# A state-space mixer rewritten: from a pipeline over chunks of 128 tokens to all chunks of 64 tokens at once

## The chip, the cores and the metric

The kernel runs on one core of one Trainium2 chip. The metric is the device time of one execution in microseconds, the median of several runs. Engines are named as in the profile: PE (TensorE matmul), PEld (TensorE weight load), DVE (VectorE), ACT (ScalarE), POOL (GpSimd), SP (SyncE, which here issues DMAs only).

## The reference, cut to what matters

The input is 8 images of 32x32 pixels and 128 channels in float32, or 8 sequences of 1024 tokens. Layer 0 is an attention over group-normalised tokens. Layer 1 adds a state-space mixer and then a spectral filter. Only the mixer is changed. It is computed twice for each sequence, forwards and backwards, each direction with its own weights, and both outputs are added:

```
z, xbc, dt = split(x @ in_proj, [256, 256 + 384])   # x: layer-normed tokens, 128 channels
xbc = silu(causal_conv4(xbc) + conv_b)
xh, Bm, Cm = split(xbc, [256, 256 + 64])            # 4 heads of 64; state size 64
dt = softplus(dt + dt_bias);  A = -exp(A_log)
# for each head, a linear recurrence over the tokens, written in chunks of CHUNK = 64:
#   Y_diag: inside a chunk,  C_l . B_s * exp(sum of dt*A from s+1 to l) * (xh*dt)_s,  s <= l
#   states: what a chunk adds to the 64x64 state, decayed to the chunk's end
#   Y_off : C_l . (state before the chunk) * exp(sum of dt*A up to l)
y  = Y_diag + Y_off + xh * D
yg = y * silu(z)
out = (yg * rsqrt(mean(yg^2) + 1e-5) * norm_w) @ out_proj
```

The result doesn't depend on the length of a chunk.

## The kernel before, in words

`fast_kernel` goes through stages, each with its own pools of SBUF and PSUM tiles: group norm and q, k, v of all images; attention (`scores`, `weigh`, `total`, `project`); the mixer; then the spectral filter in several stages (`spectra`, `matrices`, `apply`, `gather`, `back`). The tokens of all sequences stay in SBUF tiles `X[b]`, 128 tokens on the partitions and 8 blocks of tokens. A second program, `general_kernel`, follows for inputs outside a range that the fast one can handle; it isn't entered here and isn't changed.

A scheduling layer takes the written program, keeps its order as priority, gives out tile buffers and sets semaphores. So instructions of one engine may stand in another order than in the text, but each engine works through its own list in order.

The mixer has 16 units, one for each sequence and direction, direction 0 before 1. For a unit, `inputs` makes what the scan needs:

- once per sequence, `tokens`: layer norm, transposes to channels on partitions (`bxt`), the matmul for dt (`pd`), softplus in small DVE and ACT steps, `da` = dt*A;
- the decays `dec` (`pe`, L638, and an exponential);
- the projection of the 384 convolved channels in three tiles (`pp`, L654), each followed by a copy to `xp` and a scaled copy to `xs` or `bc` on ACT and three multiply-adds on DVE (L670);
- `z` with tokens on partitions (`pz`, L679), and the Silus (L694 to L697).

`scan` then does one chunk of 128 tokens at a time: transposes of x and B (`sx`), `xdt` on DVE, `xd`, `dau` and `xdd` on POOL, the segment sums `pl` (L735) and their exponential `lm` (L737), C.B (`pg`), its mask and product with `lm` (L742, L743), the new state (`pst`, L753, then POOL and DVE L758, L759), the outputs `sy` inside the chunk (L764) and from the state (L766), their sum and gate (L768 to L772), the sum of squares and `rms`, transposes back (`pyt`, L782) and the output matmul `spo` (L789) added to `X` (L790). The state goes from chunk to chunk.

The order is written out by hand: `scan` is a generator with four parts, and the chunks run as a pipeline, also across the end of a unit, with one part of the next unit's `inputs` behind each chunk:

```
            for n in range(NT):
                running = step([scan(b, d, n, made, state)] + running)
                for _ in range(2 if n == 0 else 1):
                    next(ahead, None)
```

PSUM is split among tags: `p` (one buffer of two banks, for `pp`, `pz`, `px`), one buffer each for `yt`, `x`, `seq` and `y`, two for `g`.

Of the kernel before, what the change touches and what calls it, by code (L numbers as in the profile page):

```python
# [8 lines left out]
F32 = mybir.dt.float32  # L9
# [5 lines left out]
P = 128  # L15
# [7 lines left out]
KC = 4  # L23
KF = 16
# [13 lines left out]
def fast_kernel(ctx: ExitStack, tc: tile.TileContext, a: dict, out: bass.AP, bad: bass.AP):  # L38
# [41 lines left out]

    row_le = triangle("row_le", -1, 1, 0)
    row_ge = triangle("row_ge", 1, -1, 0)
    row_lt = triangle("row_lt", -1, 1, -1)
    row_gt = triangle("row_gt", 1, -1, -1)
# [32 lines left out]
    win, cw, cb, wo, dsk = [], [], [], [], []  # L117
# [4 lines left out]
    def load_ssm_weights():  # L122
        for d, pre in enumerate(("L1_attn_fwd_", "L1_attn_bwd_")):
            w = ctile([P, 2 * DI + 2 * DS], f"win{d}")
            nc.sync.dma_start(w, a[pre + "in_proj"][:, : 2 * DI + 2 * DS])
            nc.sync.dma_start(wdt[:, d, :], a[pre + "in_proj"][:, 2 * DI + 2 * DS :])
            win.append(w)
            t = ctile([P, 3, KC], f"cw{d}")
            nc.sync.dma_start(t, a[pre + "conv_w"].rearrange("(n p) k -> p n k", p=P))
            cw.append(t)  # L130
            t = ctile([P, 3, 1], f"cb{d}")
# [4 lines left out]
            t = ctile([P, NH], f"dsk{d}")  # L136
            nc.sync.dma_start(t, a[pre + "D"].partition_broadcast(P))
            dsk.append(t)
# [209 lines left out]
    with ExitStack() as s:  # L348
        keepq = s.enter_context(tc.tile_pool(name="a_q", bufs=1))
        qs, ks, vs = [], [], []  # L350
        with ExitStack() as s2:
# [79 lines left out]
            load_ssm_weights()  # L431
# [72 lines left out]
        def project(b, half, av, pd):  # L504
# [4 lines left out]
            ot = p1.tile([P, 512], F32, tag="ot", name=f"ot{b}_{half}")  # L509
# [57 lines left out]

    with ExitStack() as s:
        p1 = s.enter_context(tc.tile_pool(name="b_1", bufs=1))
        p2 = s.enter_context(tc.tile_pool(name="b_2", bufs=2))  # L570
        p3 = s.enter_context(tc.tile_pool(name="b_3", bufs=3))
        ps_p = s.enter_context(tc.tile_pool(name="b_ps_p", bufs=1, space=PSUM))
        ps_1 = s.enter_context(tc.tile_pool(name="b_ps_1", bufs=1, space=PSUM))
        ps_2 = s.enter_context(tc.tile_pool(name="b_ps_2", bufs=2, space=PSUM))

        n2 = 2 * NH

        def tokens(b, seq):

            xn = layer_norm(p1, b, "b")  # L580
            px = ps_p.tile([P, T], F32, tag="p", name=f"px{b}")
            for j in range(NT):
                nc.tensor.transpose(px[:, j * P : (j + 1) * P], xn[:, j, :], ident)
            xt = p2.tile([P, T], F32, tag="xt", name=f"bxt{b}")
            nc.scalar.copy(xt, px)
# [3 lines left out]
            pd = ps_1.tile([P, NT * n2], F32, tag="yt", name=f"pd{b}")  # L589
            for j in range(NT):  # L590
                nc.tensor.matmul(
                    pd[:, j * n2 : (j + 1) * n2],
                    lhsT=xt[:, j * P : (j + 1) * P],
                    rhs=wdt.rearrange("p d h -> p (d h)"),
                    start=True,
                    stop=True,
                )
# [9 lines left out]
            nc.vector.tensor_tensor(v, pd.rearrange("p (j n) -> p j n", j=NT), wide(dtb), ALU.add)  # L607
# [17 lines left out]
        def inputs(b, d, seq, made):  # L625
# [5 lines left out]
            heads = slice(d * NH, (d + 1) * NH)  # L631
            upto, after = (row_le, row_gt) if d == 0 else (row_ge, row_lt)

            pe = ps_1.tile([P, 3, NT * NH], F32, tag="yt", name=f"pe{tag}")
            dac = p2.tile([P, NT, NH], F32, tag="dac", name=f"dac{tag}")
            nc.gpsimd.tensor_copy(dac, da[:, :, heads])
            for i, m in enumerate((upto, after, ones)):
                nc.tensor.matmul(  # L638
                    pe[:, i, :], lhsT=m, rhs=dac.rearrange("p j h -> p (j h)"), start=True, stop=True
                )  # L640
            dec = p2.tile([P, 3, NT, NH], F32, tag="dec", name=f"dec{tag}")
            nc.scalar.activation(
                dec.rearrange("p i j h -> p (i j h)"), pe.rearrange("p i n -> p (i n)"), AF.Exp
            )
            yield
# [3 lines left out]
            bc = p1.tile([P, T], F32, tag="bc", name=f"bc{tag}")  # L649
            pad = KC - 1  # L650
            for n, acc in ((0, xs[:, 0, :]), (1, xs[:, 1, :]), (2, bc)):
                pp = ps_p.tile([P, T], F32, tag="p", name=f"pp{tag}_{n}")
                for i in range(2):
                    nc.tensor.matmul(  # L654
                        pp[:, i * 512 : (i + 1) * 512],
                        lhsT=win[d][:, DI + n * P : DI + (n + 1) * P],
                        rhs=xt[:, i * 512 : (i + 1) * 512],
                        start=True,
                        stop=True,
                    )  # L660
# [6 lines left out]
                )  # L667
                for i in range(pad):
# [6 lines left out]
            zs = p2.tile([P, NT, DI], F32, tag="zs", name=f"zs{tag}")  # L675
            for j in range(0, NT, 4):
                pz = ps_p.tile([P, 4, DI], F32, tag="p", name=f"pz{tag}_{j}")
                for i in range(4):
                    nc.tensor.matmul(  # L679
                        pz[:, i, :],  # L680
                        lhsT=xt[:, (j + i) * P : (j + i + 1) * P],
                        rhs=win[d][:, 0:DI],
# [3 lines left out]
                nc.vector.tensor_copy(  # L686
                    zs[:, j : j + 4, :].rearrange("p j c -> p (j c)"), pz.rearrange("p j c -> p (j c)")
                )
                yield


            bt = p2.tile([DS, T], F32, tag="bt", name=f"bt{tag}")
            ct = p2.tile([DS, T], F32, tag="ct", name=f"ct{tag}")
            nc.scalar.activation(bt, bc[0:DS, :], AF.Silu)  # L694
            nc.scalar.activation(ct, bc[DS : 2 * DS, :], AF.Silu)
            for t in (xs.rearrange("p n t -> p (n t)"), zs.rearrange("p j c -> p (j c)")):
                nc.scalar.activation(t, t, AF.Silu)  # L697
            made.update(dt=seq["dt"], dec=dec, dac=dac, xs=xs, bt=bt, ct=ct, zs=zs)

        def split(t):  # L700
            return t.rearrange("p (h c) -> p h c", h=NH)

        def per_head(t, n=P):
            return t.unsqueeze(2).to_broadcast([n, NH, HP])

        def scan(b, d, n, made, state):

            dec, dac, xs, bt, ct = (made[k] for k in ("dec", "dac", "xs", "bt", "ct"))
            heads = slice(d * NH, (d + 1) * NH)
            upto, after = (row_le, row_gt) if d == 0 else (row_ge, row_lt)  # L710
            j = n if d == 0 else NT - 1 - n
            tag = f"{b}_{d}_{j}"
            cols = slice(j * P, (j + 1) * P)

            px = ps_1.tile([P, DI + DS], F32, tag="x", name=f"sx{tag}")
            for i in range(2):
                nc.tensor.transpose(px[:, i * P : (i + 1) * P], xs[:, i, cols], ident)
            nc.tensor.transpose(px[:, DI:], bt[:, cols], ident[:DS, :DS])
            xb = p2.tile([P, DI + DS], F32, tag="xb", name=f"xb{tag}")
            nc.scalar.copy(xb, px)  # L720
            xh = split(xb[:, :DI])
            xdt = p2.tile([P, DI], F32, tag="xdt", name=f"xdt{tag}")
            nc.vector.tensor_tensor(split(xdt), xh, per_head(made["dt"][:, j, heads]), ALU.mult)  # L723
# [1169 lines left out]
```

## Time and profile before

| | us |
|---|---|
| median of 3 runs | 1970.18 (1969.39 to 1972.31) |
| the profiled execution, own time | 1988.78 |
| its span | 1987.1 |
| mean granted TensorE clock | 0.918 |
| group norm, q, k, v (0 to 124) | 124, clock 0.88 |
| attention (124 to 511) | 387, clock 0.99 |
| mixer, start (511 to 548) | 37, clock 0.76 |
| mixer, units (548 to 1501) | 953, clock 0.90 |
| spectral filter (1501 to 1987) | 486 |

The profiled execution is 0.9% longer than the median of the runs; durations are taken from it. In a line of the timeline the first number is the start of a group of like instructions in us from the start of the span, the second is the time to the end of the last of them. A line of a group names line, engine and operation, output<-inputs, shapes and count. A line of waits reads: engine and its instruction, what it waited for, us in total, times, longest us. In a line of windows the numbers behind the length are busy us (and instructions) of PE, PEld, DVE, ACT and POOL, then the granted clock, the busy share of the DMA engines and GB/s.

### The profile page before, as it was taken

What the parts mean: (1) busy time and instruction counts of PE and PEld (TensorE: products, weight loads), DVE (VectorE), ACT (ScalarE), POOL (GpSimd) and SP (SyncE); (2) the same over time, 40 slices, a digit from 0 to 9 for tenths busy, and PEclk for the clock granted to TensorE, in tenths of its full rate; (3) what the DMA queues carried; (4) which work ended last, traced back from release to release, by engine and by line L of the source; (5) the groups of instructions that cost most, each with busy time, mean ns of one, the idle gap of its engine ahead of it and who ended that gap; (6) DMA issues with size and microseconds to landing.
All of it is one profiled execution on the core that took longest, in us unless ns stands there. A gap on an engine that the chain in (4) does not pass through costs nothing. (4 is left out here: it accounts for less than half of the span.)

```text
span 1987.1 us, 38739 instructions
## 1 busy us (share of the span) xinstructions
PE 1758.5 (88%) x15734; PEld 1060.3 (53%) x15734; DVE 1370.0 (69%) x2427; ACT 1051.9 (53%) x1646; POOL 1033.4 (52%) x1335
## 2 busy tenths in 40 slices
PE   5689999999699899898988999989896889999996
PEld 3432222222355565555655556555555788777772
DVE  6757677666777767877678776877764447767764
ACT  2346666666475646656465564656635325444440
POOL 5348885000277666776666766766675552323220
PEclk7899999999798979989899898988987889999998
DMA  4011111000000000000000000000003851122118
GB/s 112 1 32 55 56 57 32 1 1 1 0 1 1 12 1 1 12 0 12 1 1 11 1 11 1 1 12 0 11 1 128 226 167 57 62 64 64 62 44 305
DMA packets 80835, 80.21 MB, mean 40 GB/s; under 512 B 7272, under 2 KB 65000, under 8 KB 79624
## 3 DMA queue, kind: packets, MB, share of 16 engines
q1 hardware_dynamic: 78536, 73.45, 12.1%
q10 hardware_dynamic: 2112, 4.19, 0.6%
q8 instruction: 126, 2.06, 0.4%
q14 instruction: 61, 0.50, 0.1%
HBM read 44.08 MB, written 33.55 MB: 39 GB/s over the span
## 5 line engine op out<-in xcount | busy, mean ns | idle before, releaser
L461 ACT ACTIVATE pr<-pt 128x1024 f32<-128x1024 f32 x256 | 248.1, 1021 | 125.8 <-PE pt L456 93.0
L973 ACT COPY gs<-pg 128x512 f32<-128x512 f32 x256 | 137.4, 589 | 174.8 <-PE pg L960 159.2
L485 DVE TENSOR_TENSOR two<-pr,pr 128x1024 f32<-128x1024 f32 x128 | 162.2, 1298 | 95.3 <-PE pd L496 95.3
L971 DVE COPY gs<-pg 128x512 f32<-128x512 f32 x256 | 164.6, 684 | 88.6 <-PE pg L960 83.8
L960 PE MATMUL pg<-taps,mst 32*128 32x128 f32 x4096 | 169.7, 294 | 27.1 <-DVE gs L971 20.7
L764 PEld LDWEIGHTS sy<-xdt,lm 128*128 128x128 f32 x1024 | 141.9, 212 | 75.1 <-issue 32.5
L764 PE MATMUL sy<-xdt,lm 128*128 128x64 f32 x1024 | 154.6, 299 | 24.6 <-DVE y L771 24.1
L960 PEld LDWEIGHTS pg<-taps,mst 32*128 32x128 f32 x4096 | 142.3, 194 | 57.6 <-DVE gs L971 23.4
L456 PE MATMUL pt<-q,k 32*128 32x512 f32 x1024 | 160.6, 643 | 4.8 <-DVE taps L332 3.5
L725 POOL TENSOR_TENSOR xd<-xb,dsk 128x256 f32<-128x256 f32 x128 | 118.8, 928 | 70.8 <-DVE y L771 42.6
L476 PE MATMUL po<-pr,v 128*32 128x512 f32 x1024 | 148.7, 603 | 0.0
L670 DVE SCALAR_TENSOR_TENSOR xs<-xp,cw,xs 128x1024 f32<-128x1024 f32 x96 | 145.8, 1525 | 2.5 <-ACT xs L665 2.5
L995 PE MATMUL py<-gs,u 128*32 128x128 f32 (+1 forms) x4096 | 140.9, 281 | 0.5 <-ACT half L1007 0.5
L982 POOL COPY u<-us 128x512 f32<-128x512 f32 x16 | 17.1, 1068 | 220.4 <-issue 208.8
L663 POOL MEMSET xp<- 128x3 f32 x48 | 4.6, 98 | 216.3 <-PE pf L548 186.6
L995 PEld LDWEIGHTS py<-gs,u 128*32 128x32 f32 (+1 forms) x4096 | 105.3, 105 | 16.0 <-issue 1.5
L771 DVE TENSOR_TENSOR y<-sy,xd 128x256 f32<-128x256 f32 x128 | 53.9, 421 | 82.2 <-POOL xd L769 69.7
L456 PEld LDWEIGHTS pt<-q,k 32*128 32x128 f32 x1024 | 52.8, 184 | 103.1 <-PE pt L456 40.2
L654 PE MATMUL pp<-bxt,win 128*128 128x512 f32 x192 | 101.1, 645 | 3.6 <-ACT xs L665 2.9
L746 POOL TENSOR_TENSOR xdd<-xdt,dec 128x256 f32<-128x256 f32 x112 | 89.6, 800 | 27.0 <-DVE xdt L723 24.7
L728 POOL TENSOR_TENSOR dau<-row_le,dac 128x512 f32<-128x512 f32 x64 | 75.3, 1178 | 53.5 <-PE pl L735 53.5
L743 DVE TENSOR_TENSOR lm<-lm,gm 128x512 f32<-128x512 f32 x128 | 101.8, 795 | 2.0 <-ACT lm L737 1.0
(271 smaller groups left out, 4031.4 us busy)
## 6 DMA issues: line engine op xcount, KB each, us to landing
ud<-sp SPq DMA_DIRECT2D x8, 1024.0 KB
us<-ud SPq DMA_DIRECT2D x16, 512.0 KB
yd<-sums SPq DMA_DIRECT2D x32, 256.0 KB
yt<-yd SPq DMA_DIRECT2D x6, 1024.0 KB
X<-in_x SPq DMA_DIRECT2D x8, 512.0 KB
part_p<-in_L_ffn_M_phi_plus SPq DMA_DIRECT2D x32, 128.0 KB
part_m<-in_L_ffn_M_phi_minus SPq DMA_DIRECT2D x32, 128.0 KB
xd<-X SPq DMA_DIRECT2D x8, 512.0 KB
```

Of the source, the lines that this page charges most:

```text
L456: nc.tensor.matmul(pt[:, i, :], lhsT=k[rows, j * P : (j + 1) * P], rhs=q[rows, cols], start=True, stop=True)
L461: nc.scalar.activation(pr[:, 2 * g : 2 * g + 2, :].rearrange("p i t -> p (i t)"), pt.rearrange("p i t -> p (i t)"), AF.Exp,)
L476: nc.tensor.matmul(po[rows, :], lhsT=vs[b][:, j, rows], rhs=pr[:, h, :], start=(j == 0), stop=(j == NT - 1))
L485: nc.vector.tensor_tensor(two, sums["pr"][:, 2 * g : 2 * g + 2, :], pr[:, 2 * g : 2 * g + 2, :], ALU.add)
L670: nc.vector.scalar_tensor_tensor(acc, xp[:, at : at + T], cw[d][:, n, i : i + 1], acc, ALU.mult, ALU.add)
L725: nc.gpsimd.tensor_tensor(split(xd), xh, per_head(dsk[d]), ALU.mult)
L743: nc.vector.tensor_tensor(lm, lm, gm.unsqueeze(1).to_broadcast([P, NH, P]), ALU.mult)
L764: nc.tensor.matmul(py[:, 0, hc], lhsT=lm[:, h, :], rhs=xdt[:, hc], start=True, stop=True)
L960: nc.tensor.matmul(pts[g][:, e, :], lhsT=mst[rows, n * 4 + e, :], rhs=taps[rows, cols].rearrange("p f q m i -> p (f q m i)"), start=True, ...
L971: nc.vector.tensor_copy(to, frm)
L973: nc.scalar.copy(to, frm)
L995: nc.tensor.matmul(py[t * 32 : t * 32 + 32 - 16 * m, q, :], lhsT=u[:, i, f, q, m:].rearrange("p k i b -> p (k i b)"), rhs=mats[:, f, q, m, ...
```

## The change

The mixer is written anew for chunks of 64 tokens (`L = 64`): two chunks stand on the 128 partitions, at 0 to 63 and 64 to 127, and each operation covers all 16 chunks of a unit.

- `scan` becomes `mixed`, which runs once for each unit. Units don't overlap except for `inputs` of the next, of which one part follows each part of `mixed`. All PSUM tiles have two banks and one tag with four buffers (`wide_psum`).
- Segment sums use a mask of 64 columns, half as many elements. The decay of C is no longer a factor on tokens after the matmul: exponentials `ec` with channels on partitions come from matmuls with ones (`pe`) and are multiplied by C.
- Matmuls of B, C, states and outputs become 64x64 tiles of the array: B back to tokens (`sb`), C.B (`pg`), states (`pst`), outputs inside a chunk and from the state (`sy`). Outputs have channels on partitions and are summed in PSUM: the D term first, as a matmul with a diagonal matrix `skip`, then the terms inside the chunk, then those from the states.
- The states of 15 chunk ends are a chain of DVE operations of 64 columns, two to a step; those that the other half of the partitions needs go there by four DMAs into `moved`.
- z has channels on partitions and its Silu reads PSUM. y needs no transpose; its sum of squares is a matmul of the squares with one column of ones.
- B and C are convolved in the projection: four matmuls with weights multiplied by the taps (`wbc`), made at the start by eight POOL products from two more loads each.
- Layer norm of the mixer is applied by ACT in place of DVE. D is loaded by four small DMAs per direction. `ot` of the attention is written over `av`. The store of `X[b]` to `xd` stands at the end of a sequence's second unit.

```diff
-    row_lt = triangle("row_lt", -1, 1, -1)
-    row_gt = triangle("row_gt", 1, -1, -1)
+    upto = []
+    for d, m in enumerate((row_le, row_ge)):
+        t = ctile([P, L], f"upto{d}")
+        for c in range(2):
+            rows = slice(c * L, (c + 1) * L)
+            nc.gpsimd.tensor_copy(t[rows, :], m[rows, rows])
+        upto.append(t)
+    after = [triangle("row_gt", 1, -1, -1), triangle("row_lt", -1, 1, -1)]
+    nc.gpsimd.memset(after[0][L:, :L], 0.0)
+    nc.gpsimd.memset(after[1][:L, L:], 0.0)
...
+            w = pool.tile([P, P], F32, tag="w_bc", name=f"w_bc{d}")
+            nc.sync.dma_start(w, proj[:, 2 * DI : 2 * DI + 2 * DS])
+            rows = pool.tile([P, P, KC], F32, tag="rows_bc", name=f"rows_bc{d}")
+            nc.sync.dma_start(rows, taps_bc[DI:].partition_broadcast(P))
+            t = ctile([P, KC, P], f"wbc{d}")
+            for k in range(KC):
+                nc.gpsimd.tensor_tensor(t[:, k, :], w, rows[:, :, k], ALU.mult)
...
-            ot = p1.tile([P, 512], F32, tag="ot", name=f"ot{b}_{half}")
+            ot = av
...
+        ps_w = s.enter_context(tc.tile_pool(name="b_ps", bufs=4, space=PSUM))
...
+            dau = p1.tile([P, NT, NH, L], F32, tag="dau", name=f"dau{tag}")
+            nc.gpsimd.tensor_tensor(
+                dau,
+                upto[d].unsqueeze(1).unsqueeze(1).to_broadcast([P, NT, NH, L]),
+                da[:, :, d * NH : (d + 1) * NH].unsqueeze(3).to_broadcast([P, NT, NH, L]),
+                ALU.mult,
             )
...
+            pb = wide_psum(f"pb{tag}", (T,))
+            for i in range(2):
+                for k in range(KC):
+                    at = i * 512 + (k if d == 0 else 2 * pad - k)
                     nc.tensor.matmul(
+                        pb[:, i * 512 : (i + 1) * 512],
+                        lhsT=wbc[d][:, k, :],
+                        rhs=xt[:, at : at + 512],
...
+            pes = [wide_psum(f"pe{tag}_{r}", (NT, 2, L)) for r in range(2)]
+            for i in range(2):
+                for c in range(2):
+                    for r in range(2):
+                        rows = slice(c * L, (c + 1) * L)
+                        nc.tensor.matmul(
+                            pes[r][rows, 4 * i : 4 * i + 4],
+                            lhsT=ones[rows, :L],
+                            rhs=dau[rows, 4 * i : 4 * i + 4, 2 * r : 2 * r + 2, :],
...
+            pss = [wide_psum(f"pst{tag}_{c}", (NT, 2, HP)) for c in range(2)]
+            for j in range(NT):
+                for c in range(2):
+                    for r in range(2):
+                        rows = slice(c * L, (c + 1) * L)
+                        nc.tensor.matmul(
+                            pss[c][r * L : (r + 1) * L, j],
+                            lhsT=bk[rows, j, :],
+                            rhs=xdd[rows, j, 2 * r : 2 * r + 2, :],
...
+            for k, (j, c) in enumerate(chunks[:-1]):
+                if k == 0:
+                    nc.vector.tensor_copy(state[:, 0], pss[c][:, j])
                 else:
+                    for h in range(2):
+                        nc.vector.scalar_tensor_tensor(
+                            state[:, k, h, :],
+                            state[:, k - 1, h, :],
+                            dec[:, c, j, h : h + 1],
+                            pss[c][:, j, h, :],
...
+                        nc.sync.dma_start(
+                            moved[to, ks[0] // 2 : ks[-1] // 2 + 1],
+                            state[r * L : (r + 1) * L, ks[0] : ks[-1] + 1 : 2],
+                        )
...
+            pys = [wide_psum(f"sy{tag}_{c}", (2, NT, L)) for c in range(2)]
+            for c in range(2):
+                for n in range(2):
+                    nc.tensor.matmul(
+                        pys[c][:, n],
+                        lhsT=skip[d][:, n, :],
+                        rhs=xs[:, n, :].rearrange("p (j c l) -> p c j l", j=NT, c=2)[:, c],
...
+            for j in range(NT):
+                for r in range(2):
+                    for c in range(2):
+                        rows = slice(c * L, (c + 1) * L)
+                        for h in range(2):
+                            nc.tensor.matmul(
+                                pys[c][h * HP : (h + 1) * HP, r, j, :],
+                                lhsT=xdt[rows, j, 2 * r + h, :],
+                                rhs=lm[rows, j, 2 * r + h, :],
...
+                        for h in range(2):
+                            nc.tensor.matmul(
+                                pys[c][h * HP : (h + 1) * HP, r, j, :],
+                                lhsT=state[rows, k, h, :] if r == c else moved[rows, k // 2, h, :],
+                                rhs=ec[rows, r, j, h, :],
...
+            for n in range(2):
+                sq = p2.tile([P, T], F32, tag="sq", name=f"sq{tag}_{n}")
+                nc.scalar.activation(sq, y[:, n, :], AF.Square)
+                sqs.append(sq)
+            yield
+            for j in range(NT):
+                for n in range(2):
+                    nc.tensor.matmul(
+                        pss[:, j : j + 1],
+                        lhsT=sqs[n][:, j * P : (j + 1) * P],
+                        rhs=ones[:, 0:1],
...
-            state = {}
-            for n in range(NT):
-                running = step([scan(b, d, n, made, state)] + running)
-                for _ in range(2 if n == 0 else 1):
-                    next(ahead, None)
+            for _ in mixed(b, d, made):
+                next(ahead, None)
             for _ in ahead:
                 pass
             made = coming
```

Between these stand, in `mixed`, `pl` and `lm` (two PSUM tiles of 1024 columns), the decays `pdec`, the transposes `sx` and `xdt`, `sb` and its copy `bk` on ACT, `pg`, `xdd` and the product of `lm` with the masked C.B (`gm`), all on DVE where they are elementwise; and behind the sums of squares `rms` on POOL, the 16 output matmuls `spo` and 8 additions to `X` on DVE.

## The prediction

> **What bounds the kernel now.** I read the page first, then busy time by stage (windows), the waits and the timeline of one unit. A unit is one sequence and direction of the mixer; there are 16.
>
> ```profile
> span 1987.1 us, 38739 instructions
> ## 1 busy us (share of the span) xinstructions
> PE 1758.5 (88%) x15734; PEld 1060.3 (53%) x15734; DVE 1370.0 (69%) x2427; ACT 1051.9 (53%) x1646; POOL 1033.4 (52%) x1335
> ```
>
> ```profile
> 511.00:548.00 37.00, 26.65 (x87) 15.74 (x87) 28.37 (x89) 19.11 (x21) 13.88 (x19) 0.76 0.00 1
> 548.00:1501.00 953.00, 869.26 (x3795) 543.21 (x3793) 700.32 (x1336) 552.75 (x928) 655.79 (x894) 0.90 0.02 5
> ```
>
> The columns are stretch, length, then PE, PEld, DVE, ACT and POOL busy, granted clock, DMA. The mixer is the 953 us from 548 to 1501, 59.6 us a unit, with PE busy 91% of it and DVE 73%. The DMA chain that ends the page lies after the change. PE's waits in this stretch:
>
> ```profile
> PE sy L764 <- DVE y L771: 24.1, 33, 1.5
> PE pst L753 <- POOL xdd L746: 20.6, 27, 1.6
> PE pst L753 <- POOL rms L103: 5.8, 13, 0.6
> ```
>
> These are small, so PE nearly sets the pace. Busy PE is not PE at its peak, so I price PE by distances between starts:
>
> ```profile
> 1247.65 1.02 PE L735 MATMUL pl<-dau,row_lt 128*128 128x512 f32 x2
> 1248.51 1.03 PE L679 MATMUL pz<-win,bxt 128*128 128x256 f32 x4
> 1249.37 0.61 PE L789 MATMUL spo<-wo,yts 128*128 128x128 f32 x4
> ...
> 1254.49 1.10 PE L764 MATMUL sy<-xdt,lm 128*128 128x64 f32 x8 [0.84 <-DVE y L771]
> 1255.53 0.70 PE L766 MATMUL sy<-state,ct 64*128 64x256 f32 x2
> ```
>
> A float32 matmul is two records. 512 columns take 0.86 us (1247.65 to 1248.51), 256 take 0.43; four of 64 columns with 128-wide weights take 1.04, 0.26 each, hardly less than one of 128 columns (0.22 to 0.27)[...]. Transposes are one record, 0.11 us. Narrow tiles behave otherwise:
>
> ```profile
> 1700.26 1.08 PE L995 MATMUL py<-gs,u 128*32 128x128 f32 x32
> 1701.27 1.17 PE L960 MATMUL pg<-taps,mst 32*128 32x128 f32 x32
> 1702.37 1.08 PE L995 MATMUL py<-gs,u 128*32 128x128 f32 x32
> ```
>
> Here 16 matmuls take 1.01 or 1.10 us, so four on four different tiles take 0.25 together, what one takes alone. Last, the granted clock:
>
> ```profile
> 955.10:958.60 3.50, 2.42 (x13) 1.27 (x12) 2.99 (x8) 2.14 (x6) 3.18 (x6) 1.00 0.00 0
> 965.40:968.80 3.40, 3.40 (x25) 2.59 (x23) 2.22 (x8) 0.80 (x2) 2.13 (x5) 0.99 0.00 0
> 968.80:972.20 3.40, 3.40 (x10) 1.77 (x9) 3.13 (x7) 1.25 (x4) 3.31 (x4) 0.50 0.00 0
> ```
>
> The clock is 1.0 or 0.5 in such pieces. The mixer's mean of 0.90 is a fifth of the time at half, 12 us a unit. It drops after pieces filled with small matmuls and gaps, though PE counts as busy.
>
> [...] the median of `two` is 1224. [...] the yd store at the end of the chain took 2.19.
>
> **The change part by part, for one unit.**
>
> *PE work before:* a step, all read in the same way, is sx 0.57, pl 0.86, pg 0.41, pst 0.58, sy 1.04 and 0.62, pyt 0.28, spo 0.54, in all 4.9, times 8 less a pst and a sy, 38; xBC projections 6 x 0.86 = 5.2, pz 3.4, decays 0.7, tokens 1.3. Sum 48.6 at full clock.
>
> *PE work after, full array:* pp 4 x 0.86, bc projection with the convolution in its weights 8, pz 4, pl 4, skip 4: 24 x 0.86 = 20.6; 16 transposes 1.7; 3 decays 0.7; 16 sums of squares of one column at 0.22, 3.5; 16 output matmuls 3.5; tokens 1.3. Sum 31.3. *64x64 tiles:* ones matmuls 8 of 512 columns, on two tiles in pairs of the same tile: 3.4 if all pair, 6.9 if none; I take 4.5. pst 8 groups of four at 0.25, 2.0. The 16 diagonal and 15 state groups have 64 columns: between 0.13 and 0.25, I take 0.13: 4.1. sb and pg 8 pairs each: 2.0. [...] Total 45 at full clock; were the tiles one after another at 0.22, 32+64+60+32 matmuls would be 41 instead of 8, and the total 80. So PE's work hardly falls; the 4-fold bc projection (+5.2) eats what tiles save.
>
> *Other engines:* POOL loses xd, xdd, dau per step and yo's sum (most of its 41 us a unit) and keeps dau, 2048 elements, four times 1.04 = 4.2, hidden a unit ahead. ACT loses most table loads (1.28 each, 53+30+15 of them); after: 16 passes near 1 us, bt/ct 2.4, two loads, 25 in all, not bounding. DVE: 9 convolution steps become 6 (1.27 each), zs copies go; total 34.
>
> *The path.* The pipeline across chunks goes. `mixed` holds four 2-bank PSUM buffers and single lm, xdt, state and y, so units don't overlap: only `inputs` of the next lies between. In the order in which the changed program stands, a unit is a chain:
> - head: pl 3.4, ones 4.5, then decays 0.7, a pp 1.7, sx 0.9, each behind the other in PE's queue (ec's exponentials, 2 x 1.02, run beside), to the first xdt: 11.3 with a hand-over.
> - DVE: xdt, xdd, lm 6 x 1.22, gm 0.68, six convolution steps of the next unit in between 7.6, first state 0.3, then 14 dependent steps of two 64-column operations. X L790, 128 columns from PSUM, is 0.34; half the columns less 0.07 us, 0.27: 28 make 7.6. Sum 23.5. PE does pst, pb, pz under this. Behind each DVE step queue the next unit's convolutions, so ACT's Silu and pz wait with them.
> - tail: the second output buffer is a pst buffer, free only at the last state; skip 1.7, diagonal 2.1, states 2.0 (the DMAs of `moved`, 2.2, land under the first two; on SP nothing else is queued but the xd store), y 2 x 1.22, square 1.05, then sums and output 7.0, hand-overs between engines 8 x 0.15. Sum 17.5.
>
> Together 52.3; where tokens of the next sequence come in, px 0.9, pd 1.8 and the softplus go ahead of the convolutions, +3.3, so 54.0 on average, at full clock.
>
> *Clock.* In the tail PE is idle for y and square (3.5), then does one-column matmuls (3.3): two pieces that earn half clock. Nothing here shows this pattern; bounds 0 and 20 us at half, of which half is lost. I take 10, so +5.0: 59.0 a unit.
>
> *Ends of the stage.* Silu of the first xs ended at 542 in the trace, so the first xdt, at 11.3 of its chain, puts its start at 531. The last unit has no next: 7.6 of convolutions and 2 of waits less. End: 531 + 16 x 59.0 - 10 = 1465 against 1501, -36.
>
> *Elsewhere.* The weight products, 8 on POOL at about 0.5 (wo, double size, 0.7), and 8 more issues on SP (0.45 each) stand in the first 40 us, ahead of POOL's rsqrt of the next image. POOL has gaps of 3 to 4 us there: +2, bounds 0 and 6. The skip tables and chunk rows, some 2 us on POOL ahead of the first layer norm, are inside the rounding of 531. `ot` in `av`: the next copy into av comes 8 score steps (23 us) later, so 0. xd stores: one per sequence before and after, 0.
>
> Sum: -34 on the profiled execution's own 1988.8, or 1955; the median of the runs, 1970.2, is 0.9906 of it, so 1936.
>
> **The rivals.** A measurement tells 0.2% from no change, 4 us.
> 1. *Clock and hand-overs eat it* (slower). Break-even is (1501 + 10 - 531 - 2)/16 = 61.1 a unit, 7.1 above the full-clock chain: 14 us at half clock in PE's head and tail. The before has 12. For: the idle tail is longer than any wait now, and only one unit is in flight. Against: 512-column matmuls fill the middle. With 10 lost, 64, +46: 2015.
> 2. *The 64x64 tiles overlap only by halves* (slower). Chain +7 for diagonal, states and ones: 66, +78: about 2047; with no overlap +23, near 2300. For: not in the trace; the order mixes r and c. Against: 32-wide tiles overlap fully both ways.
> 3. *The clock holds* (faster): 55 a unit, -98: 1873.
> 4. *Nothing moves:* PE's total is 45 against 49 and PE is the bound anyway; within 4 us.
>
> **How the numbers follow.** Likeliest case 0.37 (1936; own range 1890 to 1962), rival 3 0.15, rival 1 0.32, rival 2 0.11, rival 4 0.05. So faster 0.52, same 0.05, slower 0.43. Range 1855 to 2050: it leaves out no overlap, and a unit under 54.
>
> **What would show it.** Right: POOL under 10% in the mixer; diagonal and state matmuls at about 0.13 a group; 28 state operations in 7 to 8 us; PE idle 3 to 4 us ahead of each ss; half clock just behind. Wrong: units overlapping in the output stage, groups of four at 0.4 or more, state operations over 0.35 each, or a mixer under 860 or over 1010 us.

## The result, and the profile after

The changed kernel takes **1997.38 us** (median of 4 runs, 1992.89 to 1999.45) against 1971.24 for the kernel before (4 runs, 1969.39 to 1973.48): a ratio of 1.0129, 95% interval 1.0108 to 1.0150. It is slower by 26 us, where 34 us faster was forecast. Its profiled execution has a time of its own of 1997.43, the same as its median.

The page of the kernel after, its span and the first two engines:

```profile
span 1995.7 us, 46229 instructions
## 1 busy us (share of the span) xinstructions
PE 1722.7 (86%) x20470; PEld 1079.4 (54%) x20470; DVE 1129.3 (57%) x2083; ACT 850.8 (43%) x1162; POOL 485.6 (24%) x556
```

DVE lost 241 us of work, ScalarE 201, POOL 548, and PE has hardly less. PE's waits in the mixer of the kernel after (who waited for whom, us in all, times, longest):

```profile
PE ss L984 <- ACT sq L979: 53.7, 16, 3.5
PE pst L878 <- DVE xdd L867: 30.1, 9, 3.6
PE pz L754 <- ACT ct L769: 27.1, 15, 2.5
```

Together they are about twice the three waits shown of before, and the largest is of a kind that was not there: the sums of squares wait for ScalarE's Square in every unit. The windows answer for the mixer (stretch, length, PE, PEld, DVE, ACT and POOL busy, granted clock, DMA share, GB/s):

```profile
548.00:1511.00 963.00, 827.14 (x8520) 564.03 (x8518) 465.60 (x991) 344.22 (x428) 103.71 (x96) 0.84 0.06 14
```

The last X operation of the mixer ends at 1510.9, at 1501.1 before; the stage behind it lasts 485 us, 486 before. The clock is what stands out: 0.84 where it was 0.90. Summed over its pieces, 311 us of the stretch are at half, against 191. (That profile of before was a long execution. In a second one, the run before_again below, the mixer ends at 1481.9 with 132 us at half, so against an execution near the median the change costs 29 us in the mixer.) The 14 full periods from unit to unit, from the first X operation of one to that of the next, are 61.85 us on average, 19.7 of them at half clock, where the forecast had 59.0 with 10 at half.

PE's timeline at the end of one unit of the kernel after (start, length, then the operation, its tiles, the number of records, and in brackets the idle time before it), and the same time in pieces of 3.4 us:

```profile
1063.17 1.99 PE L754 MATMUL pz<-bxt,win 128*128 128x512 f32 x4 [1.21 <-ACT ct L769]
1065.00 3.60 PE L932 MATMUL sy<-xs,skip 128*128 128x512 f32 x8
1068.53 2.10 PE L944 MATMUL sy<-lm,xdt 64*64 64x64 f32 x128
...
1077.28 0.38 PE L984 MATMUL ss<-ones,sq 128*128 128x1 f32 x2 [3.40 <-ACT sq L979]
1077.52 2.40 PE L997 MATMUL spo<-wo,y 128*128 128x128 f32 x10
1079.72 6.40 PE L984 MATMUL ss<-ones,sq 128*128 128x1 f32 x30
1085.98 5.04 PE L997 MATMUL spo<-wo,y 128*128 128x128 f32 x22
```

```profile
1073.40:1076.80 3.40, 0.48 (x27) 0.34 (x16) 2.36 (x2) 0.63 (x1) 0.00 (x0) 1.00 0.02 5
1076.80:1080.20 3.40, 2.92 (x15) 2.92 (x16) 0.00 (x0) 1.37 (x2) 0.00 (x0) 0.62 0.02 5
1080.20:1083.60 3.40, 3.40 (x17) 3.40 (x18) 0.00 (x0) 0.00 (x0) 0.00 (x0) 0.50 0.00 0
1083.60:1087.00 3.40, 3.40 (x17) 3.40 (x18) 0.17 (x1) 0.00 (x0) 0.51 (x2) 0.50 0.00 0
1087.00:1090.40 3.40, 3.40 (x18) 3.40 (x18) 0.00 (x0) 0.00 (x0) 1.33 (x1) 0.50 0.00 0
```

PE stands idle for 3.4 us while y and its square are made. Then come 15 sums of squares in 6.4 us, 0.43 each where 0.22 was priced, and 11 output matmuls in 5.0 us. PE's share of busy time is full (3.40 of 3.40) and its clock is half, for some 13 us.

It comes back behind the output matmuls of 128 columns. In the traces of before and after all changes of the clock, between 1.0 and 0.5, stand on one grid: 3.41 us or a multiple of it apart. In another unit of the kernel after, cut on this grid, a piece of output matmuls alone goes before full clock, and the next unit's pl starts later:

```profile
1149.07 4.43 PE L997 MATMUL spo<-wo,y 128*128 128x128 f32 x22
1153.34 3.60 PE L788 MATMUL pl<-dau,row_gt 128*128 128x512 f32 x8
```

```profile
1149.30:1152.71 3.41, 3.41 (x17) 3.41 (x18) 0.11 (x1) 0.00 (x0) 1.83 (x2) 0.50 0.00 0
1152.71:1156.12 3.41, 3.41 (x14) 1.96 (x14) 2.16 (x8) 0.82 (x1) 0.00 (x0) 1.00 0.01 2
```

Six pieces of this kernel's grid are filled by output matmuls alone, all at 0.50, and 1.00 follows all six. The 13 pieces filled by sums of squares alone are all at 0.50, and 0.50 follows them.

### The profile page after: what moved, and what is told of

The parts are those of the page before. It is cut to its first block, busy times and chain, and to the rows that moved or that the text cites. A ratio compares the mean times of both kernels' runs of the same rounds, so it can differ in the third digit from the quotient of the medians.

```text
span 1995.7 us, 46229 instructions
## 1 busy us (share of the span) xinstructions
PE 1722.7 (86%) x20470; PEld 1079.4 (54%) x20470; DVE 1129.3 (57%) x2083; ACT 850.8 (43%) x1162; POOL 485.6 (24%) x556
## 5 line engine op out<-in xcount | busy, mean ns | idle before, releaser
L984 PE MATMUL ss<-ones,sq 128*128 128x1 f32 x512 | 109.4, 344 | 53.7 <-ACT sq L979 53.7
L984 PEld LDWEIGHTS ss<-ones,sq 128*128 128x128 f32 x512 | 109.6, 325 | 55.9 <-ACT sq L979 55.9
L732 DVE SCALAR_TENSOR_TENSOR xs<-xp,cw,xs 128x1024 f32<-128x1024 f32 x96 | 124.0, 1294 | 1.7 <-ACT xs L726 1.6
L742 PE MATMUL pb<-bxt,wbc 128*128 128x512 f32 x256 | 123.7, 632 | 0.1
L968 DVE TENSOR_TENSOR y<-sy,zs 128x1024 f32<-128x1024 f32 x32 | 37.8, 1220 | 144.7 <-PE sy L958 144.7
L925 DVE TENSOR_TENSOR ec<-ec,ct 128x1024 f32<-128x1024 f32 x32 | 58.1, 1834 | 99.5 <-ACT ec L817 99.5
L997 PE MATMUL spo<-wo,y 128*128 128x128 f32 x512 | 113.9, 413 | 0.0
L997 PEld LDWEIGHTS spo<-wo,y 128*128 128x128 f32 x512 | 107.3, 318 | 0.0
L700 POOL TENSOR_TENSOR dau<-upto,da 128x2048 f32<-128x2048 f32 x16 | 64.3, 4018 | 176.7 <-DVE da L688 99.0
L979 ACT ACTIVATE sq<-y 128x1024 f32<-128x1024 f32 x32 | 32.0, 1048 | 162.2 <-DVE y L968 162.2
```

What stands on the lines that cost most here:

```text
L732: nc.vector.scalar_tensor_tensor(acc, xp[:, at : at + T], cw[d][:, n, i : i + 1], acc, ALU.mult, ALU.add)
L742: nc.tensor.matmul(pb[:, i * 512 : (i + 1) * 512], lhsT=wbc[d][:, k, :], rhs=xt[:, at : at + 512], start=(k == 0), stop=(k == KC - 1),)
L984: nc.tensor.matmul(pss[:, j : j + 1], lhsT=sqs[n][:, j * P : (j + 1) * P], rhs=ones[:, 0:1], start=(n == 0), stop=(n == 1),)
L997: nc.tensor.matmul(po[:, j, :], lhsT=y[:, n, j * P : (j + 1) * P], rhs=wo[d][:, n, :], start=(n == 0), stop=(n == 1),)
```

## The experiments

The theory after this reading was A: the gap ahead of the sums drops the clock, and one-column matmuls do not earn it back. Its rival B: the tail is long by its own small matmuls and waits, and the clock is a bystander. Two more suspects were read from the same trace: the projection pz, whose second half waits for the Silu of ct (27.1 us in all), and the product ec*ct, which the planner (the scheduling layer) put ahead of xdt on DVE and which the forecast had left out. In the table the mixer's end and its time at half clock (from 548 on) are from each profile; the period is the mean of the 14 between the first 15 units. fill_narrow has two runs, the other changed kernels four or six. The profiled execution of alt_tail took 2000.8 us, 18 less than the median beside it. Below, forward units are those of direction 0. A unit's head runs from its first pl to its first xdt, its tail from its last state operation to its first X. A state group is the matmuls that add the states' part to one chunk's output.

| kernel | median us | ratio to before, 95% | mixer ends | at half, us | period |
|---|---|---|---|---|---|
| before, first profile | 1970.2 | 1 | 1501.1 | 191 | |
| before, second profile | 1967.7 (one run) | | 1481.9 | 132 | |
| after | 1997.4 | 1.0129 (1.0108 to 1.0150) | 1510.9 | 311 | 61.85 |
| fill_tail | 1919.4 | 0.9736 (0.9703 to 0.9769) | 1433.3 | 130 | 56.7 |
| fill_narrow | 2000.1 | 1.0160 (1.0073 to 1.0247) | 1519.7 | 314 | 62.3 |
| alt_tail | 2019.2 | 1.0271 (1.0203 to 1.0340) | 1516.0 | 306 | 61.7 |
| gate_tail | 1869.9 | 0.9487 (0.9458 to 0.9516) | 1379.2 | 120 | 52.7 |
| ec_late | 1961.8 | 0.9955 (0.9933 to 0.9978) | 1472.6 | 259 | 59.4 |
| bc_dve | 1942.3 | 0.9871 (0.9810 to 0.9932) | 1449.8 | 294 | 57.2 |
| gate_ec | 1851.0 | 0.9397 (0.9337 to 0.9458) | 1360.1 | 96 | 52.0 |
| gate_ec_bc | 1905.3 | 0.9686 (0.9654 to 0.9718) | 1417.6 | 230 | 55.1 |
| gate_ec_alt | 1828.6 | 0.9304 (0.9270 to 0.9338) | 1344.6 | 60 | 50.5 |
| dau_late | 1804.8 | 0.9176 (0.9139 to 0.9213) | 1320.3 | 35 | 49.0 |

**before_again.** The kernel before, for a second profile.

> The kernel before, unchanged, for a second profile. The forecast multiplied its sum by 0.9906 because the profiled execution of before was 18.6 us longer than the median. If that excess was an accident of one execution, this profile's own time is within 4 us of 1971 and one stage is shorter than in the first profile by about 18 us, most likely the mixer, at a clock above 0.90; the factor was then right for the kernel before and had no ground for the changed one. If profiled executions of before are always longer, it is 1985 to 1992 again, with the mixer at 953 us.

Its time was 1967.68 us. The mixer of this profile:

```profile
548.00:1482.00 934.00, 842.08 (x3788) 524.49 (x3786) 697.20 (x1330) 552.79 (x926) 651.87 (x892) 0.93 0.02 5
```

The mixer ended 19.2 us earlier, with 59 us less at half clock and hardly any other difference; the other stages agree within 2 us. So nearly all of the 18.6 us by which the first profiled execution exceeded the median was mixer time at half clock in that one execution. There was no ground to carry it over to the changed kernel as a factor.

**fill_tail.** Wide dummy matmuls in the gap, overwritten by the real output afterwards.

```diff
+            po = wide_psum(f"spo{tag}", (NT, C))
+            with tc.issue_after(last.ins):
+                for i in range(4):
+                    last = nc.tensor.matmul(
+                        po[:, 4 * (i % 2) : 4 * (i % 2) + 4].rearrange("p j c -> p (j c)"),
+                        lhsT=ident,
+                        rhs=xs[:, i // 2, (i % 2) * 512 : (i % 2) * 512 + 512],
+                        start=True,
+                        stop=True,
+                    )
```

Here last is the last matmul of the state groups; `issue_after` fixes an order in one engine's queue and adds no wait.

> Changed kernel plus four dummy 512-column matmuls a unit (3.4 us of PE work at full clock, written into the output buffer before the real output overwrites it), queued between the last state group and the sums of squares, where PE is idle for 3.5 us. Theory A (the clock): the idle gap drops the clock, one-column matmuls cannot earn it back, so sums and output run at half. Then with the gap filled the 16 sums of squares take about 3.6 us instead of 6.8, last state group to first X operation shrinks by 3 to 5 us, and the kernel takes 1920 to 1955 although it does 55 us more matmul work. Theory B (the clock is a bystander; small matmuls and the planner's order make the tail long): 1993 to 2010, sums still above 6 us.

It took 1919.4 us, 78 less than the changed kernel, with 55 us more matmul work at full clock. PE's timeline at the end of a unit (L984, spo from xs, are the dummies), and pieces of it:

```profile
1033.81 3.17 PE L984 MATMUL spo<-xs,ident 128*128 128x512 f32 x7
...
1037.96 4.06 PE L994 MATMUL ss<-ones,sq 128*128 128x1 f32 x30
1041.88 5.47 PE L1006 MATMUL spo<-wo,y 128*128 128x128 f32 x24
```

```profile
1034.20:1037.60 3.40, 3.40 (x14) 1.81 (x13) 1.34 (x2) 1.97 (x2) 0.00 (x0) 1.00 0.02 5
1037.60:1041.00 3.40, 3.40 (x31) 3.40 (x30) 0.00 (x0) 0.03 (x1) 0.00 (x0) 0.93 0.00 0
1041.00:1044.40 3.40, 3.40 (x17) 3.40 (x18) 0.17 (x1) 0.00 (x0) 1.84 (x2) 0.50 0.00 0
```

The sums took 4.1 us instead of 6.4. From the last state group to the first X operation it is 12.8 us on average instead of 17.1; over the mixer 181 us less at half clock went with 78 us less time, 0.43 us for each. That is theory A, and B is out. The last piece adds something: there was no gap, and yet the clock fell right behind the run of one-column matmuls. That run is a cause of its own. On the clock's grid this trace has 25 pieces at full clock that sums and output matmuls alone fill, some 30 records each. Half clock followed all 11 with at least 20 records of sums, and none of the 14 with at most 19. (The border is not quite sharp: in gate_tail it followed one piece with 17, but not two with 20.)

**fill_narrow.** The same place, sixteen one-column dummies instead of four wide ones.

```diff
-                for i in range(4):
+                for i in range(16):
...
-                        rhs=xs[:, i // 2, (i % 2) * 512 : (i % 2) * 512 + 512],
+                        rhs=xs[:, 0, i : i + 1],
```

> Same place as the four wide dummy matmuls, but sixteen one-column dummies a unit (0.22 us each, 3.5 us). Now PE is busy in the gap and nothing streams. Theory A in the form 'the clock follows what is streamed': nothing is regained, sums of squares still near 0.43 us each, the kernel at 1990 to 2005. Theory A' ('the clock follows idle time alone'): as with the wide dummies, 1915 to 1930.

It took 2000.1 us. PE's timeline, then a piece behind it:

```profile
1016.04 5.57 PE L984 MATMUL spo<-xs,ident 128*128 128x1 f32 x32
1021.47 2.48 PE L1006 MATMUL spo<-wo,y 128*128 128x128 f32 x10
```

```profile
1016.00:1019.40 3.40, 3.40 (x26) 3.36 (x23) 2.31 (x2) 1.00 (x2) 0.00 (x0) 0.74 0.02 5
1019.40:1022.80 3.40, 3.40 (x17) 3.40 (x17) 0.00 (x0) 1.00 (x2) 0.00 (x0) 0.50 0.00 0
```

PE is recorded as busy without a break, and the clock drops as it does over the gap (0.74 in the piece that starts with the dummies, then 0.50; from the start of the gap it was 1.00, 0.62, 0.50). With the wide dummies it held (1.00 in the piece from 1034.20 of fill_tail), so in these runs it goes with how many columns are streamed through the array, 2048 in the wide dummies of a unit and 16 in the narrow ones, and not with busy time: PE busy for 3.40 of 3.40 us was not enough here.

**alt_tail.** Each sum of squares is followed by one output matmul, the order written out.

```diff
+            before = None
+                    for out, lhs, rhs in (
+                        (pss[:, j : j + 1], sqs[n][:, cols], ones[:, 0:1]),
+                        (po[:, j, :], y[:, n, cols], wo[d][:, n, :]),
+                    ):
+                        with ExitStack() as order:
+                            if before is not None:
+                                order.enter_context(tc.issue_after(before.ins))
+                            before = nc.tensor.matmul(out, lhsT=lhs, rhs=rhs, start=(n == 0), stop=(n == 1))
```

> Changed kernel with the 16 sums of squares (one column) and the 16 output matmuls (128 columns) issued strictly in turn, nothing else changed. Of a pair about half the time is streaming. Theory A: the gap of 3.5 us still drops the clock for the first piece, but no piece of the tail is empty of streaming, so full speed comes back after 3.4 us instead of 10 or more: 3 to 4 us a unit, 1930 to 1950. Rival: a share of a half is not enough to get full speed back, the whole tail stays at half, 1990 to 2010.

It took 2019.2 us; the rival was right, and the time lies above its range. Once the gap has dropped the clock, pairs that stream about half of the time did not bring it back (the half is an estimate: 128 columns, at 0.86 us for 512, are 0.22 of the 0.44 us from pair to pair at full clock in gate_ec_alt, below): the turns took 11 to 12 us a unit, 9 to 10 of them at half. All 23 pieces of the clock's grid that hold such pairs alone are at half, and half follows them. The planner put one matmul of the next pl among the turns. In five units the clock came back early, behind a piece with pl and pairs; in others such a piece was not enough.

**gate_tail.** The next unit's pz and its Silu behind this unit's last state group: real work in the gap.

```diff
-                pzs.append(pz)
...
+            def gate(behind):
...
+                        order.enter_context(tc.issue_after(behind.ins))
...
+                        nc.scalar.activation(zs[:, n, :], pz, AF.Silu)
+            made["gate"] = gate
...
+            if "gate" in coming:
+                coming["gate"](last)
             pss = wide_psum(f"ss{tag}", (NT,))
```

> Changed kernel with the next unit's pz projection and its Silu moved from behind pb to behind this unit's last state group. Theory A: pz (3.7 us) and its wait for the Silu of ct (2 us) leave the stretch between pb and skip, and real work fills the gap that drops the clock: 8 to 10 us a unit, the kernel at 1835 to 1880. Theory B: only the middle shortens and the tail stays as long, about 5 us a unit: 1910 to 1930. Theory C (skip and diagonal wait for the state chain on DVE anyway, and the Squares now stand behind zs on ScalarE): no gain, 1985 to 2000.

It took 1869.9 us, 127 less than the changed kernel. PE's timeline:

```profile
1003.15 3.71 PE L768 MATMUL pz<-bxt,win 128*128 128x512 f32 x8
1007.34 0.38 PE L990 MATMUL ss<-ones,sq 128*128 128x1 f32 x2 [0.47 <-ACT sq L985]
1007.58 2.25 PE L1003 MATMUL spo<-wo,y 128*128 128x128 f32 x18
1009.67 3.41 PE L990 MATMUL ss<-ones,sq 128*128 128x1 f32 x30
1012.94 1.81 PE L1003 MATMUL spo<-wo,y 128*128 128x128 f32 x14
```

The gap is half a microsecond, the sums are at 0.23 each. The stretch from the last state operation to the last state group fell from 10.0 us to 5.6, the rest of the tail from 17.1 to 12.6: both halves of the expectation, and of about equal size.

**ec_late.** The product ec*ct held behind the state chain on DVE.

```diff
-            for r in range(2):
+            with tc.issue_after(tail.ins):
+              for r in range(2):
```

Here tail is the last operation of the state chain.

> Changed kernel with the two multiplications ec*ct held behind the last state operation on DVE; as planned they stand ahead of xdt, where one of them takes 3.7 us in forward units beside the 3.6 us of dau on POOL. Theory D (the head is set by them): xdt starts 2.5 us earlier in forward units and 1.2 in backward ones, and 2.5 us at the end of the state chain lie under skip and diagonal: about 1.5 to 2.5 us a unit, 1955 to 1975. Theory E (PE's pb, pz and skip set when the output groups can start): the gain is lost as a longer wait behind pb, 1990 to 2000.

It took 1961.8 us, 36 less than the changed kernel, as theory D said, but not by its split: forward units fell from 61.3 to 56.5 us from pl to X, backward ones stayed at 63.0. In forward units the head lost 2.5 us and the stretch from the last state operation to the last state group 2.4. What the forward units had is seen in the changed kernel on DVE and POOL:

```profile
1037.57 4.81 DVE L925 TENSOR_TENSOR ec<-ec,ct 128x1024 f32<-128x1024 f32 x2 [6.46 <-ACT ec L817]
1042.31 1.21 DVE L842 TENSOR_TENSOR xdt<-sx,dt 128x1024 f32<-128x1024 f32 x1
```

```profile
1036.55 3.62 POOL L700 TENSOR_TENSOR dau<-upto,da 128x2048 f32<-128x2048 f32 x1 [10.40 <-PE pe L808]
```

The first of the two products lasted 3.67 us, until 1.1 us after dau had ended on POOL; xdt, whose transposes were done, waited behind both.

**bc_dve.** One part of the change undone: B and C go through one tap of projection and are convolved on DVE again.

```diff
-            for n in range(2):
-                acc = xs[:, n, :]
+            for n in (0, 1, 2):
+                acc = xs[:, n, :] if n < 2 else bc
...
-            pb = wide_psum(f"pb{tag}", (T,))
```

> One part of the change undone: the convolution of B and C back on DVE (three operations of 1.27 us, two ScalarE passes) and their projection back to one tap, so PE loses 5.2 us a unit at full clock and DVE gains 3.8. Theory F (PE's queue pb, pz, skip sets when the output groups start): the stretch from pst to the last state group shortens by 0 to 3 us, 1950 to 1997. Theory G (DVE's chain of xdd, lm, convolutions and state sets it): 3 to 4 us a unit longer, 2040 to 2060.

It took 1942.3 us, 55 less than the changed kernel and a little below the range of theory F: in the order of the changed program pb, pz and skip were on the path, not under the state chain.

**gate_ec.** Both moves that gained: the diffs of gate_tail and ec_late together.

> Both moves that gained alone: pz and its Silu behind the last state group, ec*ct behind the state chain. Alone they gave -127 and -36 us. If they act on different stretches (tail and middle against head) the gains add: 1830 to 1845. If holding ec*ct back now lengthens the end of the state chain, since pz no longer stands between pb and skip to cover it, only part of the 36 comes: 1850 to 1870.

1851.0 us: 19 of the 36 came on top. In forward units the head fell to 11.1 us; at the end of the state chain PE now waits for ec*ct, 17.7 us in all.

**gate_ec_bc.** The two moves and the diff of bc_dve, so the fold of B and C is undone.

> The two gaining moves plus the B and C convolution back on DVE. With the tail filled PE is busy 93% of the mixer and is the bound, so 5.2 us less of it a unit should show: with all of it 1770, with the part that DVE's 3.8 us more and its waits for the convolution leave, 1800 to 1830. Rival: the fold was the cover of the state chain on DVE; without it PE waits there, 1845 to 1880.

1905.3 us, 54 slower than gate_ec and beyond the range of its rival, though PE has 47 us less busy time. PE's waits in its mixer (us, times, longest):

```profile
PE sy L947 <- DVE ec L914: 88.9, 32, 8.0
PE sy L921 <- ACT bc L722: 24.0, 7, 3.6
```

With the tail filled, the fold is the work that covers DVE's state chain. Without it PE waits for the chain and ec*ct, and more of the time is at half clock: 230 us against 96. The same edit gained 55 us in one order and lost 54 in another.

**gate_ec_alt.** The two moves and the diff of alt_tail, the strict turns.

> The two gaining moves plus strict turns of sums of squares and output matmuls. Turns did nothing where the clock was already down. If a half share of streaming holds full speed though it cannot regain it, the piece at half behind the sums (1.5 to 2 us a unit in the profile with pz moved) goes: 0.5 to 1 us a unit, 1835 to 1845. If a half share is too little to hold it as well, the tail drops within the turns: 1860 to 1890.

1828.6 us, better than expected. From the last state group to X there is 0.2 us at half instead of 3. A half share of streaming held the full clock where it had not been able to regain it: 15 pieces of the clock's grid hold pairs alone, all at full clock (33 records at 1.00 in the 3.40 us from 1043.60), and full clock follows them. Taking turns is not needed for that, only the share in a piece: the 14 pieces of fill_tail that held it had sums and outputs in runs. How much of the 22 us the clock gave is open, since the order changed as well. The planner put part of the next pl among the turns: from the first X to the next xdt it is 3.9 us less, from the last state group to X 2.2 more.

**dau_late.** In addition da and dau of the next sequence behind ec*ct.

```diff
+            if "decays" in coming:
+                with tc.issue_after(tail.ins):
+                    coming["decays"]()
```

The line that it aims at, in gate_ec_alt:

```profile
1014.99 4.44 DVE L732 SCALAR_TENSOR_TENSOR xs<-xp,cw,xs 128x1024 f32<-128x1024 f32 x1
1019.35 3.91 DVE L908 SCALAR_TENSOR_TENSOR state<-state,dec,pst 128x64 f32<-128x64 f32 x20
```

```profile
1013.82 4.53 POOL L700 TENSOR_TENSOR dau<-upto,da 128x2048 f32<-128x2048 f32 x1 [4.82 <-PE pp L715]
```

> The version with both moves and strict turns, and in addition da and dau of the next sequence held behind ec*ct. In the profiles so far dau (3.6 to 4.5 us on POOL) falls beside an operation of DVE with both sources in SBUF, which then takes 3.7 to 4.4 us in place of 1.2; in the backward units this stands ahead of the state chain. If the two really take turns, the backward units (55.8 us against 49.3 for the forward ones) lose 2 to 3 us each: 1800 to 1815. If the long operation is hidden behind PE's queue, nothing: 1823 to 1834.

**1804.8 us**, the fastest: 0.9176 of the kernel before (0.9139 to 0.9213). The periods that end with a backward unit fell from 53.8 to 50.6 us; those of forward units stayed at 47.3 and 47.5. Its groups:

```profile
L703 POOL TENSOR_TENSOR dau<-upto,da 128x2048 f32<-128x2048 f32 x15 | 54.3, 3620 | 57.3 <-PE pe L819 32.9 <-DVE da L689 24.4
L937 DVE TENSOR_TENSOR ec<-ec,ct 128x1024 f32<-128x1024 f32 x32 | 37.7, 1220 | 0.0
```

All dau are at 3.62 us and all ec*ct at 1.22; in the changed kernel they were 4.05 and 1.83 on average.

## Why the prediction was wrong

The miss is 61 us: 42 in the sum for the profiled execution (1997.4 against 1955) and 19 in the factor.

**The terms of the path**, means over the second to the fifteenth unit, tokens included:

| part | forecast | measured |
|---|---|---|
| head, pl to the first xdt | 11.3 | 11.7 (10.0 backward, 13.4 forward) |
| DVE run to the last state operation, with tokens | 23.5 + 1.7 | 23.4 |
| tail to the last state group | 5.8 | 10.0 |
| tail from there to the first X | 11.7, with all hand-overs | 17.1 |
| clock, where it fell | 5.0 | inside the rows above |
| sum | 59.0 | 62.1, less 0.3 of overlap |

The 0.3 of overlap aside, the tail and the clock carry the miss: 22.5 us were forecast for them, 27.1 measured. A DVE run 1.8 us shorter than forecast made up for part of it. Two steps failed, each by some 2 to 3 us a unit, an estimate from the numbers below.

**The step that failed first: "PE does pst, pb, pz under this".** Of PE's work that was to lie under DVE's run, part stood behind its end. skip, diagonal and states were priced at 5.8 us after the last state operation and took 10.0. The second pz waits for a PSUM buffer that pb holds until the Silu of ct has read it, and skip's 3.6 us come after that. With pz moved away (gate_tail) the stretch takes 5.6; with the fold of pb undone (bc_dve) it takes 4.4. The forward units of ec_late and gate_ec, which differ in the place of pz alone, take 8.1 and 4.8. None of the rivals had this wait.

**The step that failed second: the size of the clock term.** The prediction wrote "I take 10, so +5.0", an estimate within its bounds of 0 and 20. It placed the drop rightly, in the idle tail and the one-column matmuls, and counted two pieces for it. The traces show four, 13.8 us from the last state group to X, since half clock outlasts the sums until a piece is filled by output matmuls, alone (six units) or with the next pl (nine). With the other drops 19.7 us a unit are at half, close to its bound of 20. Not half of that is lost: 17.1 against 11.7 is 5 to 6 us in the tail. Some more stands in the stretch ahead. In forward units 5.4 us of the DVE run are at half in the kernel after and none in ec_late; the run takes 20.4 in both, but the stretch behind it 10.5 and 8.1. At 0.43 for each us, as in fill_tail, 19.7 us at half are about 8.5 lost (an estimate), 3.5 over the 5.0 put in.

The outcome has the mechanism of rival 1 (slower, 2015) with a smaller loss to the clock, and beside it the wait ahead of skip.

**A term left out:** ec*ct, 2.4 us of DVE a unit and 4.8 in forward ones. The prediction read the order from the program; the planner put one of the two products ahead of the first xdt in backward units, and both in forward ones. Moving them gave 36 us. The head's total came out near only because the ones matmuls took 3.7, all paired, and not 4.5.

**The factor 0.9906.** It took 18.5 us off for an accident of one profile of the kernel before; before_again shows what the accident was.

**Smaller terms.** The first pl started at 538.9, not 531, since pb and pz of the first unit stand ahead of it in PE's queue: +8. The last unit lasted 45.9 instead of 49: -3. With 15 units at +2.75 (41) this makes the +46 of the mixer's end. The +2 of stage 0 was not seen: the attention's last po ended at 501.8, and at 503.0 and 501.2 in the two profiles of before, which differ by nearly as much. Of the 45 us of PE's work 1 us rests on no trace; it was the author's estimate.

**Right:** units do not overlap in the output stage. The 64x64 tiles overlap fully, which takes rival 2 out, as these groups of the kernel after show (busy us, mean ns of one record):

```profile
L944 PE MATMUL sy<-lm,xdt 64*64 64x64 f32 x2048 | 33.5, 220 | 0.0
L905 DVE SCALAR_TENSOR_TENSOR state<-state,dec,pst 128x64 f32<-128x64 f32 x448 | 88.9, 274 | 1.0
```

A unit's 64 diagonal matmuls of two records took 2.10 us at the timeline's 1068.53, 0.13 for each group of four, though one record lasts 0.22. The state operations took less than the 7 to 8 us named (see the end). PE idle ahead of the first ss was 3.4 us as forecast, POOL is at 10.8% in the mixer, a little over the 10% named.

## What to carry to other kernels

Ask of every piece of about 3.4 us what is streamed through PE in it, and not whether PE is busy (fill_narrow: busy 3.40 of 3.40 us, and the clock at 0.50 behind it). A gap followed by narrow matmuls cost the matmuls behind it too: an output matmul took 0.46 us in the kernel after (11 in 5.04) and 0.26 in gate_tail (7 in 1.81). Move work that is needed only later into the gap, and mix narrow matmuls with wide ones: a half share of each held a full clock (15 pieces of gate_ec_alt) but did not restore one (23 pieces of alt_tail at half), which a piece of 128-column matmuls did (six in the kernel after). Read the planned order of each engine before pricing a chain; an operation that the program writes last may run first, and a cover that is worth 55 us in one order can be a burden in another.

## What the runs showed of the hardware beyond what was expected

- **DVE and POOL took turns.** In the kernel after and gate_ec_alt a DVE operation with both tensor sources in SBUF waited for dau on POOL: 3.67 instead of 1.22 us for ec*ct, 4.44 instead of 1.28 for a convolution step. When DVE came first, dau started 0.2 us behind such a step and lasted 4.53 instead of 3.62. State operations, with one source in PSUM, stayed at 0.27 beside it (0.25 to 0.28 in the kernel after).
- **The state chain was quicker than its operations.** In forward units its 28 operations, 14 dependent steps of two halves, took 5.5 us, 0.19 us apart, though one lasts 0.274 (7.6 us were forecast, from an estimated 0.27 each). Neighbours in the queue are the two halves of a state, which don't need each other, and their records overlap. In backward units steps of the next unit's convolution lie between.
- In 12 units PE pauses once for 0.8 to 1.2 us in the middle of the state groups, put down to "issue" (12.6 us in 12 units). No run tells what it is.
